# A deeper transpose pipeline in the expert pages of layer 0: four pairs ahead instead of three

## The chip, the cores and the metric

The kernel runs on one core of one Trainium2 chip. The metric is the device time of one execution in microseconds (us). The names of the engines in the profile are PE (TensorE, matrix products), PEld (TensorE's loading of weights), DVE (VectorE), ACT (ScalarE), POOL (GpSimd) and SP (SyncE, which here only issues transfers). Each engine works through its own instructions in order and waits for the others by semaphores.

## What is computed

Two layers, each a graph step over 128 graphs of 64 nodes with 256 features (8192 tokens), followed by a mixture of experts. The change lies in the mixture of layer 0: 64 experts, 6 of them chosen for each token. Cut to that part:

```python
logits = jnp.einsum('bsd,ed->bse', x, gate_w)            # 64 experts
top_logits, indices = jax.lax.top_k(logits, 6)
scores = jax.nn.softmax(top_logits, axis=-1)
W_sel = lattice_weights[indices]                          # (64, 256, 256), one matrix per expert
xW = jnp.einsum('bsd,bskde->bske', x, W_sel)
lattice_out = jnp.einsum('bske,bsk->bse', xW, scores)
# ... then a projection, a residual and a layer norm; layer 1 follows
```

The kernel sorts instead of gathering matrices. While it computes the graph step it writes each token's row six times into a table in HBM (`r0x`), at a place in the chunk of the chosen expert. A row is 258 floats: the 256 features, the row of the answer to which the result belongs, and the score. 128 rows of one expert are a page. A page is read, transposed on TensorE, multiplied by its expert's 256 x 256 matrix (all 64 matrices lie in SBUF as `lat`), scaled by the score and written back by an indirect transfer to the table of answers (`r0y`), from which the next stage sums six rows a token.

## The kernel before

Twelve full pages, one of each of the first twelve experts, are done early, while the last rows of the table are still being sent. Their tiles are placed by hand; the tile named `space` leaves 1008 floats per partition free.

```python
    with tc.tile_pool(name="e0", bufs=1, ...) as ex, tc.tile_pool(name="e1", bufs=4, side="right", ...) as et, ...:
        early = {}
        for j in (0, 3, 2, 1, None, 4, 5):
            if j is None:
                ex.tile([P, 1008], F32, name="space")
            else:
                early[j] = ex.tile([P, 2, W], F32, name=f"early{j}")
        # ... fetch_early, flip_early, apply_early: as below, for the early pages
        for e in range(EARLY):                 # EARLY = 12
            fetch_early(e)
        staggered(EARLY // 2, ((-2, flip_early), (0, apply_early)))
```

Then come all other pages in pairs. `W` is 258, `C` is 256, `KD` is 2. `px` is the buffer of a pair's rows: it takes the fetch, is overwritten by the scaled product, and is free when the reply has read it. `pxT` holds the transposed copy.

```python
    with tc.tile_pool(name="wx0", bufs=3, reuse_waits="tile") as wx, \
            tc.tile_pool(name="pt1", bufs=4, space=PSUM, ...) as pt_pool, \
            tc.tile_pool(name="py1", bufs=4, space=PSUM, ...) as py_pool:
        ring = [wx.tile([P, KD, C], F32, name="pxT", bufs=5)]

        def fetch(j):                          # SyncE
            Q["px"] = px = wx.tile([P, 2, W], F32, name="px", bufs=22)
            for q in range(2):
                # ... the page's row number is loaded once for four pages
                r0.fetch(i, regs["row"][i % 4], px[:, q:q + 1, :])

        def flip(j):                           # TensorE, then ScalarE
            # ... 4 transposes of 128x128 into pt (PSUM)
            Q["xT"] = xT = ring.pop() if ring else wx.tile([P, KD, C], F32, name="pxT", bufs=5)
            nc.scalar.copy(xT[:, :, :n * P], pt[:, :, :n * P])

        def apply(j):                          # TensorE, VectorE, GpSimd
            if j < E0:
                r0.fill_end(j)                 # a write of 128 filler rows, issued by ScalarE
            # ... 8 matmuls of 128x256 into py (PSUM)
            for q in range(n):
                nc.vector.tensor_scalar(px[:, q, :D], py[:, q, :], px[:, q, D + 1:D + 2], None, op0=ALU.mult)
                r0.reply(2 * j + q, px[:, q, :], px[:, q, :D])     # indirect transfer, GpSimd

        stages = ((-12, fetch), (0, apply),
                  (-2, lambda j: flip(j) if j < 4 else None), (-3, lambda j: flip(j) if j >= 4 else None))
        staggered(mean_pages, stages)
        # ... more pairs, if the routing needs them
```

`staggered` runs step s over the stages in the order written: fetch of pair s+12, product of pair s, then transposes of pair s+2 (for the first four pairs) or s+3.

Of the kernel before, what the change touches and what calls it, by code (L numbers as in the profile page):

```python
# [9 lines left out]
F32 = mybir.dt.float32  # L10
# [9 lines left out]
P = 128  # L20
# [445 lines left out]
def staggered(n, stages, first=0):  # L466

    for s in range(first + min(lag for lag, _ in stages), n + max(lag for lag, _ in stages)):
        for lag, f in stages:
            if first <= s - lag < n:  # L470
                f(s - lag)
# [3 lines left out]
def two_layer_gnn_moe_kernel(ctx: ExitStack, tc: tile.TileContext, a: dict, out: bass.AP):  # L475
# [6 lines left out]
    KD = D // P  # L482
    T = 2
    C = T * P
# [75 lines left out]
    W = r0.W  # L560
# [283 lines left out]
    with tc.tile_pool(name="wx0", bufs=3, reuse_waits="tile") as wx, \  # L844
            tc.tile_pool(name="pt1", bufs=4, space=PSUM, reuse_waits="tile") as pt_pool, \
            tc.tile_pool(name="py1", bufs=4, space=PSUM, reuse_waits="tile") as py_pool:
        npair = (r0.pages + 1) // 2
        pairs = [dict() for _ in range(npair)]
        regs = {}
        ring = [wx.tile([P, KD, C], F32, name="pxT", bufs=5)]  # L850

        def fetch(j):
            Q = pairs[j]
            Q["px"] = px = wx.tile([P, 2, W], F32, name="px", bufs=22)
            for q in range(2):
                i = 2 * j + q
                if i % 4 == 0:
                    regs["row"] = r0.load(0, i, ENG.SP)
                if i < r0.pages:
                    r0.fetch(i, regs["row"][i % 4], px[:, q:q + 1, :])  # L860

        def flip(j):
            Q = pairs[j]
            pt = pt_pool.tile([P, KD, C], F32, name="pt")
            n = min(2, r0.pages - 2 * j)
            for q in range(n):
                for k in range(KD):
                    nc.tensor.transpose(pt[:, k, ts(q, P)], Q["px"][:, q, ts(k, P)], ident)  # L868
            Q["xT"] = xT = ring.pop() if ring else wx.tile([P, KD, C], F32, name="pxT", bufs=5)
            nc.scalar.copy(xT[:, :, :n * P], pt[:, :, :n * P])  # L870

        def apply(j):
            Q = pairs[j]
            if j < E0:
                r0.fill_end(j)
            if j % 2 == 0:
                regs["e"] = r0.load(1, 2 * j, ENG.PE)
            py = py_pool.tile([P, 2, D], F32, name="py")
            px, xT = Q["px"], Q["xT"]
            n = min(2, r0.pages - 2 * j)  # L880
            for q in range(n):
                for k in range(KD):
                    nc.tensor.matmul(py[:, q, :], lhsT=xT[:, k, ts(q, P)],  # L883
                                     rhs=lat[:, ds(regs["e"][(2 * j + q) % 4], 1), k, :].rearrange("p o d -> p (o d)"),
                                     start=(k == 0), stop=(k == KD - 1))
            for q in range(n):
                nc.vector.tensor_scalar(px[:, q, :D], py[:, q, :], px[:, q, D + 1:D + 2], None, op0=ALU.mult)  # L887
                r0.reply(2 * j + q, px[:, q, :], px[:, q, :D])


        stages = ((-12, fetch), (0, apply),
                  (-2, lambda j: flip(j) if j < 4 else None), (-3, lambda j: flip(j) if j >= 4 else None))
        likely = (r0.likely_pages - EARLY + 3) // 4 * 2

        mean_pages = (K0 * N // P + E0 // 2 - EARLY) // 4 * 2
        staggered(mean_pages, stages)
        wait = const.tile([1, 4], F32, name="wait")
        with tc.If(r0.needed(2 * mean_pages)):
            staggered(likely, stages, mean_pages)
            with tc.If(r0.needed(2 * likely)):  # L900
                staggered(npair, stages, likely)

                nc.sync.dma_start(out=wait, in_=r0.answer[0:1, 0:4])
# [7 lines left out]
    wx = ctx.enter_context(tc.tile_pool(name="wx1", bufs=2, side="right", reuse_waits="tile"))  # L911
# [317 lines left out]
```

## Time and profile before

| | |
|---|---|
| time, median of three runs | 2074.68 us (2069.03 to 2075.51) |
| span of the profiled execution | 2434.4 us |
| mean granted clock of TensorE in it | 0.927 |
| busy in it: PE, PEld, DVE, ACT, POOL | 84%, 72%, 49%, 41%, 47% |
| stage of layer 0's pages in it (first transpose to last product) | 845.4 to 1469.3 us |
| copies `pxT` / replies `r0y<-px` in that stage | 202 / 404 |

The profiled execution is one run with a recording of every instruction; its span is longer than the time without a recording, so its shares and orders are used, and its sums with care. A line of the costliest groups gives: source line, engine and operation, output<-input, count, then busy time and the mean of one in ns, then the idle time of the engine just before these instructions and what ended most of it. A line of the timeline gives: start, duration, engine, source line, operation, output<-input and count, and in brackets the idle time of the engine before it with its releaser. "issue" means that the profile shows nothing waited for; "remote" that the releaser is not known.

### The profile page before, as it was taken

To read this page: it belongs to the slowest core of one execution; us is meant where nothing else is said; L and a number is where in the kernel's file an instruction comes from. 1 tells how busy PE (TensorE), PEld (TensorE's weight loads), DVE (VectorE), ACT (ScalarE), POOL (GpSimd) and SP (SyncE) were. 2 spreads that over 40 slices of the span, in tenths; PEclk is the share of its full clock that TensorE was granted. 3 is DMA by queue.
4 is the path that set the end of the run, shared out by engine and by line. 5 is a ranking of instruction groups with operands and counts; after the bars stand their busy time and mean duration, and the time that the engine had idled before them with its cause. 6 is when DMAs were issued, how large, how long until landed. Compare 5 with 4: busy or idle time off the path is not lost. (4 is left out here: it accounts for less than half of the span.)

```text
span 2434.4 us, 36827 instructions
## 1 busy us (share of the span) xinstructions
PE 2043.7 (84%) x10516; PEld 1750.1 (72%) x10516; DVE 1184.6 (49%) x3981; ACT 1009.9 (41%) x2033; POOL 1144.3 (47%) x1134
## 2 busy tenths in 40 slices
PE   7887878878876578778787877888988899999997
PEld 6776767767665467666666765777777788888886
DVE  5677657667765622222222224777778422222221
ACT  5765656656655112111111212555555333333332
POOL 0345444554555656666666661233333444444443
PEclk9999889989898689889999888999999899999998
DMA  3223333433234678765555526887774476666665
GB/s 109 91 99 113 125 118 106 131 122 119 101 108 157 196 234 234 218 181 176 174 170 174 160 80 242 289 267 239 248 235 138 128 181 162 162 159 165 160 167 101
DMA packets 282557, 397.88 MB, mean 163 GB/s; under 512 B 56025, under 2 KB 236393, under 8 KB 282353
## 3 DMA queue, kind: packets, MB, share of 16 engines
q1 hardware_dynamic: 202880, 246.61, 34.5%
q0 software_dynamic: 64416, 136.14, 18.8%
q10 hardware_dynamic: 15056, 12.69, 1.6%
q8 instruction: 94, 1.54, 0.3%
q14 instruction: 111, 0.90, 0.1%
HBM read 222.84 MB, written 176.64 MB: 164 GB/s over the span
## 5 line engine op out<-in xcount | busy, mean ns | idle before, releaser
L314 POOL DMA_INDIRECT r0x<-xs,r0row x384 | 385.6, 1004 | 442.3 <-issue 343.3
L883 PE MATMUL py<-lat,pxT 128*128 x1616 | 427.9, 412 | 114.2 <-ACT pxT L870 86.0
L321 POOL DMA_INDIRECT r0y<-px x404 | 392.3, 971 | 230.9 <-DVE px L887 107.2
L883 PEld LDWEIGHTS py<-lat,pxT 128*128 128x128 f32 x1616 | 317.2, 207 | 169.7 <-ACT pxT L870 97.9
L887 DVE TENSOR_SCALAR px<-py,px 128x256 f32<-128x256 f32 x404 | 170.9, 478 | 453.2 <-PE py L883 160.9
L331 POOL DMA_INDIRECT out_x<-py_s,px x138 | 214.6, 1555 | 294.3 <-DMA out_x<-py_s,px 136.8
L870 ACT COPY pxT<-pt 128x512 f32<-128x512 f32 x202 | 113.9, 588 | 515.3 <-remote 161.9
L696 PE MATMUL ps<-lat 128*128 128x256 f32 x1024 | 267.2, 412 | 15.6 <-issue 14.4
L1167 ACT ACTIVATE phid<-ph,pw 128x256 f32<-128x256 f32 x276 | 130.9, 474 | 322.6 <-issue 211.3
L663 PE MATMUL ph<-lat 128*128 128x256 f32 x1024 | 243.8, 396 | 20.6 <-issue 14.3
L1165 PE MATMUL ph<-pxT,pw 128*128 128x256 f32 x1104 | 251.1, 381 | 0.7 <-ACT pxT L1156 0.7
L696 PEld LDWEIGHTS ps<-lat 128*128 128x128 f32 x1024 | 213.1, 211 | 53.5 <-issue 17.9
L1185 PE MATMUL py<-fw,phid 128*128 (+1 forms) x1104 | 249.7, 379 | 0.0
L663 PEld LDWEIGHTS ph<-lat 128*128 128x128 f32 x1024 | 201.1, 199 | 53.6 <-issue 19.4
L1165 PEld LDWEIGHTS ph<-pxT,pw 128*128 128x128 f32 x1104 | 210.7, 191 | 29.9 <-ACT pxT L1156 1.1
L1185 PEld LDWEIGHTS py<-fw,phid 128*128 128x128 f32 x1104 | 204.5, 190 | 25.0
L314 POOL DMA_INDIRECT r1x<-xs,r1row x128 | 126.2, 986 | 202.1 <-DVE bn_rs L1004 114.2
L666 ACT ACTIVATE lat<-ph,c_L_gnn_b 128x256 f32<-128x256 f32 x256 | 102.5, 471 | 113.1 <-remote 52.9
L868 PE MATMUL pt<-ident,px 128*128 128x128 f32 x808 | 132.3, 285 | 7.7 <-issue 7.6
L868 PEld LDWEIGHTS pt<-ident,px 128*128 128x128 f32 x808 | 107.7, 149 | 33.9 <-issue 14.0
L685 DVE SCALAR_TENSOR_TENSOR lat<-ph,c_L_gnn_b,rms 128x256 f32<-128x256 f32 x256 | 103.1, 475 | 52.3 <-ACT rms L59 45.7
L1188 DVE TENSOR_TENSOR py_s<-py,pb 128x512 f32<-128x512 f32 x69 | 47.8, 692 | 155.4 <-PE py L1185 155.4
(303 smaller groups left out, 2872.1 us busy)
## 6 DMA issues: line engine op xcount, KB each, us to landing
px<-r0x SPq DMA_DIRECT2D x404, 129.0 KB
y<-r0y SPq DMA_DIRECT2D x64, 768.0 KB
pw<-in_L_ffn_W1b SPq DMA_DIRECT2D x69, 514.0 KB
px<-r1x SPq DMA_DIRECT2D x69, 258.0 KB
x<-x SPq DMA_DIRECT2D x64, 256.0 KB
pb<-in_L_ffn_b SPq DMA_DIRECT2D x69, 128.0 KB
r0x<-r0filler ACTq DMA_DIRECT2D x64, 129.0 KB
lat<-in_x SPq DMA_DIRECT2D x32, 256.0 KB
```

Of the source, the lines that this page charges most:

```text
L314: i = self.nc.gpsimd.indirect_dma_start(out=self.table[:, :], out_offset=bass.IndirectOffsetOnAxis(ap=row[:, t, k:k + 1], axis=0), in_=xs[ ...
L321: d = self.nc.gpsimd.indirect_dma_start(out=self.answer[:, :], out_offset=bass.IndirectOffsetOnAxis(ap=x[:, self.D:self.D + 1].bitcast(I32 ...
L331: i, d = f"{self.name}add{i}", self.nc.gpsimd.indirect_dma_start(out=self.total[:, :], out_offset=bass.IndirectOffsetOnAxis(ap=x[:, self.D ...
L663: nc.tensor.matmul(ph[:, c, :], lhsT=w1[:, k, ts(2 * j + c, P)], rhs=B["aggT"][:, k, :], start=(k == 0), stop=(k == KD - 1))
L696: nc.tensor.matmul(B["po"][:, t, :], lhsT=B["hT"][:, c, ts(t, P)], rhs=w2[:, c, :], start=False, stop=(t == T - 1 and c == KH - 1))
L868: nc.tensor.transpose(pt[:, k, ts(q, P)], Q["px"][:, q, ts(k, P)], ident)
L870: nc.scalar.copy(xT[:, :, :n * P], pt[:, :, :n * P])
L883: nc.tensor.matmul(py[:, q, :], lhsT=xT[:, k, ts(q, P)], rhs=lat[:, ds(regs["e"][(2 * j + q) % 4], 1), k, :].rearrange("p o d -> p (o d)") ...
L887: nc.vector.tensor_scalar(px[:, q, :D], py[:, q, :], px[:, q, D + 1:D + 2], None, op0=ALU.mult)
L1165: nc.tensor.matmul(ph, lhsT=w[:, k * F1 + c * P:k * F1 + (c + 1) * P], rhs=Q["xT"][:, k, :], start=(k == 0), stop=(k == KD - 1))
L1167: nc.scalar.activation(hid[:, c, :], ph, AF.Relu, bias=w[:, KD * F1 + c:KD * F1 + c + 1], scale=1.0)
L1185: nc.tensor.matmul(py[:, t, :], lhsT=Q["hid"][:, c, ts(t, P)], rhs=fw2[:, ds(e, 1), c, :].rearrange("p o d -> p (o d)"), start=(c == 0), s ...
```

## The change

In the stage of layer 0's pages, pairs from the fifth on are transposed four pairs ahead of their product instead of three. The transposed copies are held longer, so there are seven buffers for them instead of five. The memory comes from the row buffers, 20 pairs instead of 22. It is meant to give the copies on ScalarE more time before TensorE needs them.

```diff
-        ring = [wx.tile([P, KD, C], F32, name="pxT", bufs=5)]
+        ring = [wx.tile([P, KD, C], F32, name="pxT", bufs=7)]
 
         def fetch(j):
             Q = pairs[j]
-            Q["px"] = px = wx.tile([P, 2, W], F32, name="px", bufs=22)
+            Q["px"] = px = wx.tile([P, 2, W], F32, name="px", bufs=20)
...
-            Q["xT"] = xT = ring.pop() if ring else wx.tile([P, KD, C], F32, name="pxT", bufs=5)
+            Q["xT"] = xT = ring.pop() if ring else wx.tile([P, KD, C], F32, name="pxT", bufs=7)
             nc.scalar.copy(xT[:, :, :n * P], pt[:, :, :n * P])
...
         stages = ((-12, fetch), (0, apply),
-                  (-2, lambda j: flip(j) if j < 4 else None), (-3, lambda j: flip(j) if j >= 4 else None))
+                  (-2, lambda j: flip(j) if j < 4 else None), (-4, lambda j: flip(j) if j >= 4 else None))
```

## The prediction

> **What bounds the kernel now.** I read first the costliest groups, to see which engine the page stage of layer 0 leans on.
>
> ```profile
> L883 PE MATMUL py<-lat,pxT 128*128 x1616 | 427.9, 412 | 114.2 <-ACT pxT L870 86.0
> L321 POOL DMA_INDIRECT r0y<-px x404 | 392.3, 971 | 230.9 <-DVE px L887 107.2
> L883 PEld LDWEIGHTS py<-lat,pxT 128*128 128x128 f32 x1616 | 317.2, 207 | 169.7 <-ACT pxT L870 97.9
> L870 ACT COPY pxT<-pt 128x512 f32<-128x512 f32 x202 | 113.9, 588 | 515.3 <-remote 161.9
> ```
>
> The stage runs 202 pairs of pages (202 copies, 404 replies). TensorE loses time to late copies (86.0 us of matmul idle, 97.9 us of weight-load idle, largely the same moments). This is the wait the change goes for. GpSimd's replies wait 107.2 us for VectorE. Next, the timeline of an undisturbed piece gives each engine's period.
>
> ```profile
> 1215.40 0.60 PE L868 MATMUL pt<-ident,px 128*128 128x128 f32 x4
> 1215.84 1.89 PE L883 MATMUL py<-lat,pxT 128*128 x8
> 1217.57 0.60 PE L868 MATMUL pt<-ident,px 128*128 128x128 f32 x4
> ```
>
> And the replies on GpSimd, from the entry of the stage:
>
> ```profile
> 852.14 0.97 POOL L321 DMA_INDIRECT r0y<-early  x1 [0.30 <-issue]
> 853.42 0.97 POOL L321 DMA_INDIRECT r0y<-early  x1 [0.31 <-issue]
> 857.18 0.97 POOL L321 DMA_INDIRECT r0y<-px  x1 [2.80 <-DVE px L887]
> ```
>
> TensorE starts a pair every 1217.57 - 1215.40 = 2.17 us. GpSimd starts a reply every 853.42 - 852.14 = 1.28 us, so a pair costs it 2.56 us. 202 pairs are 438 us of TensorE at full clock and 516 us of GpSimd. Without waits GpSimd is the slower of the two, even against TensorE at the mean granted clock of 0.927 (2.17 / 0.927 = 2.34 us). In the profiled run the stage took 624 us (first transpose 845.4, last product 1469.3), because ScalarE or VectorE sometimes stands still for 5 to 9 us:
>
> ```profile
> 1209.30 0.59 ACT L870 COPY pxT<-pt 128x512 f32<-128x512 f32 x1 [9.09 <-remote]
> 1209.93 3.46 PE L883 MATMUL py<-lat,pxT 128*128 x8 [3.91 <-ACT pxT L870]
> ```
>
> Nothing in the program explains 9.09 us there. The profiled span is 2434.4 us against 2074.68 us timed, so I take most of these stops to be the recording's own. That is a choice, and the prediction hangs on it: late copies then look worth up to about 180 us in the page, but far less in the timed run. They do not concentrate in the part that issues filler writes from ScalarE: TensorE's waits for pxT are 34.2 + 31.1 us in the first 200 us of the stage, 60.6 + 52.6 us in the next 400, the same share.
>
> The last view is the stage's entry.
>
> ```profile
> 838.59 3.22 DVE L836 TENSOR_SCALAR early<-py,early 128x256 f32<-128x256 f32 x8
> ...
> 839.34 0.99 POOL L321 DMA_INDIRECT r0y<-early  x1 [4.36 <-DVE early L836]
> ...
> 839.70 32.19 SPq L460 DMA_DIRECT2D px<-r0x  x28
> ...
> 845.45 0.74 PE L868 MATMUL pt<-ident,px 128*128 128x128 f32 x4
> ...
> 848.15 1.96 PE L883 MATMUL py<-lat,pxT 128*128 x8 [0.42 <-issue]
> ```
>
> The fetches of row buffers start at 839.70, beside the twelve early replies (839.34 to 853.42 + 0.97 = 854.39). So page 0 is transposed at 845.45 and multiplied at 848.15, and GpSimd, done with the early pages at 854.39, finds work prepared; what stops it until 857.18 is a standstill of VectorE.
>
> **What the Trainium skill says.** "Perfetto Trace Analysis", section "DMA Instruction — SWDGE (GPSIMD)": the profiled end is when the descriptors are made, not when the data has landed. So 0.97 us is not the reply; whoever reuses its buffer waits longer. "DMA: Bandwidth & Descriptors", section "Anatomy of one DMA — SWDGE (gpsimd) path": a fixed cost of about 2 us, most of it the receipt from the memory written. No single line here shows the landing of a reply, so I use 2 us as an estimate from that page. "Perfetto Trace Analysis", section "Optimization Strategy": gaps that repeat can mean too few buffers. This trace agrees only in part: the gaps on TensorE repeat, but their releaser is a copy that starts late, not a full ring (waits of the fetches for replies are 19.5 us over 11 times).
>
> **The change part by part.** (1) Transposes from pair 4 on come one pair earlier; no instruction is added or removed. The slack between a transpose and its product grows from three pairs (3 x 2.17 = 6.5 us) to four (8.7 us). A stop of ScalarE of 5 to 9 us is then mostly absorbed. In the timed run I give this 0 to 10 us: TensorE is ahead of GpSimd anyway, and a wait of TensorE costs only if GpSimd has emptied its backlog.
>
> (2) Row buffers 22 to 20. Fetch j+12 waits for the reply of pair j-8 instead of j-10. If GpSimd lags as computed (2.56 against 2.17 to 2.34), TensorE runs ahead until the ring stops it. Each pair of buffers less, and the transpose a pair earlier, shorten the lead it can have by 3 pairs in all, 3 x 2.56 = 7.7 us of lead lost at the end of the stage. The next stage starts when TensorE ends, while GpSimd's last replies are hidden behind its first blocks. Cost 0 to 8 us.
>
> (3) Addresses, which the diff does not show. Seven copies take 7 x 2048 = 14,336 bytes at the start of the pool instead of 10,240. In the built programs the early pages' tiles are laid out so that a gap of 1008 floats stays free. The kernel before puts the row buffer of pair 0 into that gap (address 180,992; the early tiles 4 and 5 start at 183,104 and 185,184), and the buffers that overlap those tiles come only for pairs 12, 14 and 17. In the changed program the copies fill the gap, and the row buffer of pair 0 stands at 185,088, over early tiles 4 and 5. In the order of the built programs the first fetch of a page now waits for VectorE, TensorE and the last four early replies to have landed; the queue of SyncE is in order, so every later fetch waits behind it.
>
> Worked out on the times above: the last early reply has its descriptors at 854.39 and lands at about 856.4, so the first fetch moves from 839.70 to 856.4, 16.7 us later. From issue to the first transpose it takes 845.45 - 839.70 = 5.75 us, from there to the product 2.70, then about 2.2 + 0.6 for the product and its scaling: the first reply starts near 867.7. GpSimd is free at 854.7; it stands 13 us. Next, pair 1 is multiplied only after the transposes of pair 4, which now come before it on TensorE; pair 4 is the ninth fetch, 8 x 1.15 (32.19 / 28) = 9.2 us behind the first, so near 871.4, and the replies of pair 1 begin near 876 instead of 870.3: another 5 to 6 us. From there on fetches (2.3 us a pair) are faster than GpSimd. Sum 18 to 19 us of idle GpSimd, against at most 2.8 in the trace before: about 16 us. TensorE starts about as much later. Whichever of the two sets the end, 16 us stay.
>
> **Sum.** +16 (entry) + 4 (middle of 0 to 8) - 7 (deeper slack, towards the upper end of 0 to 10 because real stops of ScalarE at its filler writes exist: 8.83 us at 913) = +13 us; 2074.7 + 13 = 2088.
>
> **Rivals.** (a) The standstills are real and the deeper transposes win. For it: 184 us of waits for pxT. Removing a third of them would give -30 us net of the entry, 2055 to 2060. Against it: the profiled span is 360 us above the timed one, and behind TensorE comes GpSimd with 516 us that no transposing order shortens. (b) The entry is hidden: if GpSimd's lag is not what ends the stage, or the early replies run later than SyncE's fetch anyway, only a few us remain: 2072 to 2078. Against it: TensorE too has nothing to do until the first page lands. (c) The ring becomes the bound: with 20 pairs and a lag of GpSimd, fetches stop for replies through the whole stage. Each stop costs TensorE, not GpSimd, whose backlog is then full; it stays within the 8 us of part 2, unless landing times under load are much longer than 2 us, then 2100 to 2110.
>
> **Range and chances.** The certain part is +16 with an error of some 5 us; the uncertain ones pull both ways by 10. Three runs of before spread over 6.5 us. I take 2071 to 2104. Two per cent are 41 us: neither way likely. Slower by that needs (c) at its worst on top of the entry, faster needs (a) in full.
>
> **What would show it.** In the changed profile the first fetch of px should start 16 to 20 us after the first early reply, not 0.4 us; GpSimd should show one gap of 12 to 15 us between the last early reply and the first px reply, and a second of about 5 us after pair 0; TensorE's idle for pxT (184 us) should fall, perhaps by half, in the profiled run. If the fetches start beside the early replies as before, part 3 is wrong. If the timed run gains more than 10 us, my taking the standstills for the recording's own is wrong.

## The result and the profile after

The changed kernel takes 2094.44 us (median of four, 2090.5 to 2098.69), the kernel before 2075.1 us: a ratio of 1.010, 95% interval 1.0073 to 1.0128, 19.3 us slower. I had said 2088, within 2071 to 2104.

The costliest groups of the changed kernel that answer to those shown of before:

```profile
L321 POOL DMA_INDIRECT r0y<-px x404 | 393.7, 975 | 134.6 <-issue 45.5
L883 PE MATMUL py<-lat,pxT 128*128 x1616 | 390.2, 385 | 16.9 <-ACT pxT L870 12.4
L870 ACT COPY pxT<-pt 128x512 f32<-128x512 f32 x202 | 117.9, 586 | 386.4 <-PE pt L868 292.1
```

TensorE's matmul idle for late copies has gone from 86.0 us to 12.4 us, and GpSimd's idle from 230.9 to 134.6 us. It looks like the hoped success, with a slower kernel. But the two recordings cannot be compared: their spans are 2434.4 and 2096.9 us, while the times go the other way by 19 us. On which chips these two were made is not known; the experiments show that chips differ by as much. The kernel before, recorded again on a chip where it takes 2076.55 us, has this:

```profile
L321 POOL DMA_INDIRECT r0y<-px x404 | 392.7, 972 | 123.2 <-DMA r0y<-px 51.2
L883 PE MATMUL py<-lat,pxT 128*128 x1616 | 390.5, 385 | 18.1 <-ACT pxT L870 14.0
L870 ACT COPY pxT<-pt 128x512 f32<-128x512 f32 x202 | 118.0, 586 | 368.3 <-PE pt L868 258.2
```

The wait that the change goes for is 14.0 us here, not 86.0. Deeper transposes make it 12.4. GpSimd's idle of 123.2 us is almost all the 0.30 us between one reply and the next (404 x 0.30 = 121); it never waits for work. From here on "before" means this recording. The two recorded runs took 2098.69 and 2076.55 us, so they lie 22 us apart where the medians lie 19.

The entry of the stage, timeline, changed kernel (start, duration, engine, line, operation; in brackets the idle time before):

```profile
675.34 0.98 POOL L321 DMA_INDIRECT r0y<-early  x1 [0.30 <-issue]
678.12 27.01 SPq L460 DMA_DIRECT2D px<-r0x  x40
680.37 2.35 PE L868 MATMUL pt<-ident,px 128*128 128x128 f32 x8 [20.76 <-DMA px<-r0x]
682.87 3.75 PE L883 MATMUL py<-lat,pxT 128*128 x8
687.41 0.97 POOL L321 DMA_INDIRECT r0y<-px  x1 [11.10 <-DMA px<-r0x]
688.69 0.98 POOL L321 DMA_INDIRECT r0y<-px  x1 [0.30 <-issue]
690.47 0.97 POOL L321 DMA_INDIRECT r0y<-px  x1 [0.80 <-DVE px L887]
```

and the kernel before:

```profile
661.53 28.28 SPq L460 DMA_DIRECT2D px<-r0x  x40
663.76 1.19 PE L868 MATMUL pt<-ident,px 128*128 128x128 f32 x4 [4.88 <-DMA px<-r0x]
667.01 3.51 PE L883 MATMUL py<-lat,pxT 128*128 x8
674.39 0.97 POOL L321 DMA_INDIRECT r0y<-early  x1 [0.30 <-DMA r0y<-early]
675.67 0.97 POOL L321 DMA_INDIRECT r0y<-px  x1 [0.30 <-issue]
```

The first fetch is issued at 678.12 instead of 661.53 (1.0 us of this arose earlier, since the first early reply starts at 661.3 instead of 660.3): 1.80 us after the last early reply's descriptors (675.34 + 0.98 = 676.32), which fits a wait for its landing. GpSimd stands 11.10 us where it stood 0.30. The waits of SyncE's own queue in the changed kernel name it (us in total, times, longest); the first line does not occur in the kernel before, the second does there with 181.4 us:

```profile
SPq L460 <- DMA r0y<-early: 15.2, 1, 15.2
SPq L460 <- DMA r0y<-px: 182.8, 133, 3.8
```

The second line is the other thing to see: page fetches wait for replies all through the stage (in the kernel before, 12 to 24 us in every 50 us from 700 to 1150). The ring of row buffers, which are used in turn, is full in both kernels, and GpSimd paces it. The next lines give durations in ns (least, median, longest) and then the start of the first and last product, and of the first and last reply; before, then changed:

```profile
L883 PE MATMUL py<-lat,pxT x1616: 379/379/767, 667.0 to 1144.9; 128*128 x180
L321 POOL DMA_INDIRECT r0y<-px x404: 967/970/1250, 675.7 to 1190.3; - x135
```

```profile
L883 PE MATMUL py<-lat,pxT x1616: 379/379/763, 682.9 to 1165.7; 128*128 x180
L321 POOL DMA_INDIRECT r0y<-px x404: 968/972/1234, 687.4 to 1203.7; - x135
```

Replies come every (1190.3 - 675.7) / 403 = 1.277 us before and (1203.7 - 687.4) / 403 = 1.281 us after. GpSimd ends 13.4 us later, TensorE 20.8 us later. TensorE's lead at the end (start of the last reply less that of the last product) is 1190.3 - 1144.9 = 45.4 us before and 38.0 us after. The next stage starts with TensorE: its first matmul moves from 1151.5 to 1171.6, and the last stage's first from 1545.5 to 1567.6. Two losses, then: the entry, and 7.4 us of lead.

### The profile page after: what moved, and what is told of

The parts are those of the page before. It is cut to its first block, busy times and chain, and to the rows that moved or that the text cites. A ratio compares the mean times of both kernels' runs of the same rounds, so it can differ in the third digit from the quotient of the medians.

```text
span 2096.9 us, 36822 instructions
## 1 busy us (share of the span) xinstructions
PE 1935.8 (92%) x10516; PEld 1679.1 (80%) x10516; DVE 1187.0 (57%) x3981; ACT 1016.9 (48%) x2033; POOL 1159.8 (55%) x1134
## 5 line engine op out<-in xcount | busy, mean ns | idle before, releaser
L314 POOL DMA_INDIRECT r0x<-xs,r0row x384 | 395.7, 1031 | 258.1 <-issue 171.1
L321 POOL DMA_INDIRECT r0y<-px x404 | 393.7, 975 | 134.6 <-issue 45.5
L883 PE MATMUL py<-lat,pxT 128*128 x1616 | 390.2, 385 | 16.9 <-ACT pxT L870 12.4
L887 DVE TENSOR_SCALAR px<-py,px 128x256 f32<-128x256 f32 x404 | 177.0, 480 | 329.5 <-PE py L883 325.6
L883 PEld LDWEIGHTS py<-lat,pxT 128*128 128x128 f32 x1616 | 294.1, 192 | 58.2 <-ACT pxT L870 16.3
L663 PE MATMUL ph<-lat 128*128 128x256 f32 x1024 | 234.1, 388 | 11.6 <-DVE lat L685 10.9
L696 PE MATMUL ps<-lat 128*128 128x256 f32 x1024 | 237.4, 380 | 0.0
L696 PEld LDWEIGHTS ps<-lat 128*128 128x128 f32 x1024 | 193.1, 191 | 24.6
L868 PEld LDWEIGHTS pt<-ident,px 128*128 128x128 f32 x808 | 100.8, 143 | 58.1 <-issue 26.2
L1179 DVE TENSOR_SCALAR p<-p 128x2 f32<-128x2 f32 x69 | 11.7, 170 | 225.5 <-ACT p L1178 225.5
L687 ACT ACTIVATE lat<-lat,c_L_gnn_rms_weight 128x256 f32<-128x256 f32 x256 | 105.7, 495 | 37.7 <-DVE lat L685 37.3
```

Source lines behind the costliest of these rows:

```text
L314: i = self.nc.gpsimd.indirect_dma_start(out=self.table[:, :], out_offset=bass.IndirectOffsetOnAxis(ap=row[:, t, k:k + 1], axis=0), in_=xs[ ...
L321: d = self.nc.gpsimd.indirect_dma_start(out=self.answer[:, :], out_offset=bass.IndirectOffsetOnAxis(ap=x[:, self.D:self.D + 1].bitcast(I32 ...
L663: nc.tensor.matmul(ph[:, c, :], lhsT=w1[:, k, ts(2 * j + c, P)], rhs=B["aggT"][:, k, :], start=(k == 0), stop=(k == KD - 1))
L696: nc.tensor.matmul(B["po"][:, t, :], lhsT=B["hT"][:, c, ts(t, P)], rhs=w2[:, c, :], start=False, stop=(t == T - 1 and c == KH - 1))
L883: nc.tensor.matmul(py[:, q, :], lhsT=xT[:, k, ts(q, P)], rhs=lat[:, ds(regs["e"][(2 * j + q) % 4], 1), k, :].rearrange("p o d -> p (o d)") ...
```

## The experiments

My theory: the loss is the late entry plus the shorter lead, and the deeper transposes bring nothing, because TensorE is ahead of GpSimd. Rivals: the ring costs all of it; or the deeper transposes do gain, under a larger loss.

**The chips.** The first runs fell on a chip where the kernel before takes 2449 us. The kernel before, recorded there:

> The kernel before, unchanged, recorded once more. Theory (the standstills of ScalarE and VectorE were the recording's own): a recording without them shows a span near 2075 us, TensorE's waits for pxT under 40 us, GpSimd's replies 1.28 us apart through the whole stage, the first page fetch 0 to 3 us after the first early reply's start, and a gap of GpSimd between the last early reply and the first px reply under 3 us. Rival (the kernel before really stands still, and the deeper transposes cured it): waits for pxT near 180 us again.

```profile
L883 PE MATMUL py<-lat,pxT 128*128 x1616 | 426.5, 411 | 115.0 <-ACT pxT L870 89.7
L870 ACT COPY pxT<-pt 128x512 f32<-128x512 f32 x202 | 113.3, 589 | 516.9 <-remote 170.6
```

Its span was 2447.3 us, and 47 timed runs of the kernel before on this chip gave 2449.15 us (2440.56 to 2460.14). TensorE's waits for `pxT` were 89.7 us in the matmuls and 102.4 us in the weight loads, near 180 as the rival said; but these are waits of the unchanged kernel, and whether the deeper transposes cure them is another question. On another chip the expectation was

> The kernel before, unchanged, recorded in the hope of a chip on which it takes 2075 us. Theory: there the recording shows a span near 2075 us, TensorE's waits for pxT under 40 us, replies of GpSimd 1.28 us apart through the whole stage, fetches of pages beside the early replies, a gap of GpSimd before the first px reply under 1 us. Rival: waits for pxT of 100 us and more, as on the other chip.

and it held: span 2074.8 us, first fetch 1.2 us after the start of the first early reply (660.3), and the groups shown above. So a recording takes as long as the timed runs of its chip, and it does not make the standstills: they went with the chip. Of the four chips of these experiments two gave 2075 us to the kernel before and two 2449 us. I compare only within a chip, with one exception that is named.

**The entry given back.** The changed kernel, with more space left free among the early tiles:

```diff
-                ex.tile([P, 1008], F32, name="space")
+                ex.tile([P, 2024], F32, name="space")
```

> The changed kernel with the space among the early tiles made 2024 floats, once more, in the hope of a chip on which the kernel before takes 2075 us. There, theory (late entry most, shorter lead the rest): 2081 to 2086, fetches beside the early replies, GpSimd without a gap. Rival (the ring costs all): 2092 to 2097. Rival (the deeper transposes gain): 2070 or below. On a chip where the kernel before takes 2449 us: no difference over 0.3%, as the first time.

2083.06 us against 2076.6: ratio 1.0031 (1.0021 to 1.0042). The first fetch is at 661.60, and GpSimd goes straight on:

```profile
674.25 0.97 POOL L321 DMA_INDIRECT r0y<-early  x1 [0.30 <-DVE px L887]
675.53 0.97 POOL L321 DMA_INDIRECT r0y<-px  x1 [0.30 <-DMA r0y<-early]
```

```profile
L883 PE MATMUL py<-lat,pxT x1616: 379/379/767, 667.2 to 1152.2; 128*128 x180
L321 POOL DMA_INDIRECT r0y<-px x404: 967/970/1242, 675.5 to 1190.2; - x135
```

GpSimd ends where it ended before (1190.2), and TensorE's lead is still 38.0 us. Of the ratio 1.010, 1.0100 / 1.0031 = 1.0069 is the entry, about 14 us; 0.0031, 6.5 us, is left. This is the exception: the two ratios were not measured side by side, and with their intervals the entry is 8 to 20 us. GpSimd's end, 13.4 us later in the changed kernel and not later here, agrees. That rules out the ring as the whole cause, and leaves the deeper transposes no gain larger than what the rows cost.

On the chip of 2449 us the same kernel gave no difference, 0.9989 (0.997 to 1.0009):

> The changed kernel with the hand-placed space among the early tiles made 2024 floats instead of 1008, so that the row buffer of pair 0 lies over no early tile; transposes four ahead, seven copies, 20 rows as changed. Theory (the late entry is most of the loss, the shorter lead the rest): about 11 us of the 19 come back, 2081 to 2086; first page fetch beside the early replies again. Rival (the shorter ring costs all of it): 2092 to 2097. Rival (the deeper transposes gain something that the entry hid): 2070 or below.

There the question of the rival was best posed, since there TensorE does wait for copies. Little of the wait is now put to the copies (15.5 us), but most of the idle time is still there:

```profile
L883 PE MATMUL py<-lat,pxT 128*128 x1616 | 432.3, 407 | 91.8 <-issue 73.9
```

The matmul idle is 91.8 us instead of 115.0, and the time is the same within -7 to +2 us. GpSimd's idle before its replies hardly moved (235.8 us against 237.0).

**The entry alone.** The kernel before without the space, so that pair 0 lies over early tiles 4 and 5:

```diff
-        for j in (0, 3, 2, 1, None, 4, 5):
+        for j in (0, 3, 2, 1, 4, 5):
```

> The kernel before with the space among the early tiles taken out, so that the row buffer of pair 0 lies over early tiles 4 and 5; three ahead, five copies, 22 rows as before. Theory (late entry): 11 to 14 us slower than before, 2086 to 2089, with a gap of GpSimd of about 11 us after the last early reply. Rival (the ring costs all): 2075, as before.

> The kernel before with the space taken out (pair 0 over early tiles 4 and 5), again, where the kernel before takes 2075 us. Theory (the late entry alone): 12 to 14 us slower than before, first page fetch about 16.6 us after its place in the kernel before, GpSimd standing 11 us, the lead of TensorE at the stage's end unchanged at 45 us. Rival (entry and lead are not additive): under 8 us or over 18.

Both fell on chips of 2449 us: ratios 1.0029 (1.0013 to 1.0045) and 1.0015 (1.0003 to 1.0027), 4 to 7 us slower. The wait and the gap themselves are as expected: SyncE's first page fetch waits 15.8 us for an early reply in both recordings, and GpSimd stands (first run)

```profile
852.64 0.97 POOL L321 DMA_INDIRECT r0y<-early  x1 [0.31 <-issue]
864.88 0.97 POOL L321 DMA_INDIRECT r0y<-px  x1 [11.27 <-DVE px L887]
```

That less than the gap reaches the end fits a GpSimd that waits anyway on these chips (237.0 us of idle before its replies in the kernel before, against 123.2 us). The number for a chip of 2075 us was not measured; there the entry's cost rests on the changed kernel with and without the wider space.

**The rows alone.** The kernel before with `px` at `bufs=20` instead of 22:

> The kernel before with 20 pairs of row buffers instead of 22 and nothing else. Theory (a pair of row buffers is 2.56 us of lead of TensorE over GpSimd at the end of the stage): 5 us slower, 2079 to 2081. Rival (the ring never fills): 2075. Rival (the ring costs all): 2090 or more.

That was the chip of 2449 us: 1.0005 (0.9991 to 1.0018), nothing. On a chip of 2075 us:

> The kernel before with 20 pairs of row buffers instead of 22 and nothing else, again. On a chip at 2075 us, theory (two pairs of 2.56 us less lead of TensorE over GpSimd at the stage's end): 4 to 6 us slower than before. Rival (the loss left in the version with the wider space comes from the deeper transposes and copies alone): no difference.

2083.96 against 2075.55 us, ratio 1.0039 (1.0028 to 1.005), 8.4 us. More than expected, and enough for all of what the wider space left over (6.5 us; the intervals overlap).

```profile
L883 PE MATMUL py<-lat,pxT x1616: 378/379/764, 667.8 to 1150.4; 128*128 x180
L321 POOL DMA_INDIRECT r0y<-px x404: 967/969/1201, 676.3 to 1191.7; - x135
```

The lead falls from 45.4 to 41.3 us, by 4.1 us, near two pairs less (2 x 2.55 = 5.1). TensorE ends 5.5 us later than before, and the last stage starts 8.5 us later (1554.0 us against 1545.5; with the wider space it starts at 1554.0 us too). So some 3 us arise in the stage between; why, these runs do not show.

**The depth alone.** Four ahead with six copies and all 22 row buffers, space at 1512 floats so that the entry stays early:

```diff
-                ex.tile([P, 1008], F32, name="space")
+                ex.tile([P, 1512], F32, name="space")
...
-                  ... (-3, lambda j: flip(j) if j >= 4 else None))
+                  ... (-4, lambda j: flip(j) if j >= 4 else None))
```

> Four pairs ahead with six copies and all 22 row buffers, the space among the early tiles at 1512 floats so that the row buffer of pair 0 lies over no early tile. Theory (a transpose one pair earlier is one pair, 2.56 us, less lead of the products; nothing is gained, since TensorE is ahead of GpSimd): 1 to 4 us slower than before. Rival (the deeper transposes gain, and only the rows cost): 3 us or more faster than before.

2076.61 against 2075.55 us, ratio 1.0002 (0.9992 to 1.0011): nothing within some 2 us either way. TensorE's wait for copies is 12.0 us here, 14.0 before:

```profile
L883 PE MATMUL py<-lat,pxT 128*128 x1616 | 388.9, 384 | 15.6 <-ACT pxT L870 12.0
```

The last product starts 1.9 us later (1146.8 against 1144.9), as one more product behind the last transpose would.

**The opposite direction.** Two ahead, four copies, 24 row buffers, early tiles in the order 0, 1, 2, 3 and a pad of 32 floats so that pair 0 stays free:

> The opposite direction: all pairs two ahead, four copies, 24 pairs of row buffers, with early tiles placed so that pair 0 lies over none of them. Theory (lead at the stage's end is rows less transposes ahead: three pairs more than before): 5 to 8 us faster than before, TensorE's end of the stage that much nearer. Rival (copies two pairs ahead come too late, above all while ScalarE issues the filler writes): slower than before by 5 us or more.

2073.98 against 2075.55 us, ratio 0.9994 (0.9982 to 1.0006): not the 5 to 8 us. TensorE's last product starts 3.6 us earlier (1141.3), but GpSimd ends later, at 1198.0: it stands for pages or products not yet there at four places of the early part (6 us together, the first of them here) and once before its last reply:

```profile
690.60 0.97 POOL L321 DMA_INDIRECT r0y<-px  x1 [1.82 <-DMA px<-r0x]
1197.97 1.07 POOL L321 DMA_INDIRECT r0y<-px  x1 [5.15 <-DVE bn_mv L46]
```

What held the last reply is not settled; VectorE is by then in the next stage. What the longer lead runs into can be seen. The kernel lets only the first five blocks of the next stage read answers before the last reply has landed, and SyncE's fetch for the sixth block waits for it (before, then two ahead; the line number is shifted by one):

```profile
SPq L939 <- DMA r0y<-px: 5.6, 1, 5.6
SPq L940 <- DMA r0y<-px: 16.2, 1, 16.2
```

That fetch starts at 1200.31 us instead of 1193.93, although TensorE ends its pages earlier. So GpSimd's last replies are not wholly hidden, even in the kernel before. Whether this wait took up the expected gain is not shown: the last stage still starts at 1544.9 us, against 1545.5.

**A version meant to beat both.** Three ahead as before, four copies, 24 row buffers, placed as in the last one:

> Three pairs ahead as before, but four copies instead of five and 24 pairs of row buffers instead of 22, with early tiles placed so that pair 0 lies over none. Theory (20 to 22 pairs was worth 8 us, one pair ahead or less under 2): TensorE ends the stage 5 us nearer, 5 to 8 us faster than before. Rival (22 pairs are enough, or four copies make the transposes wait): no difference or slower.

> Three pairs ahead, four copies, 24 pairs of row buffers, again, in the hope of a chip on which the kernel before takes 2075 us. There, theory (each pair of row buffers is lead of TensorE over GpSimd): TensorE's last product 5 us nearer, 2067 to 2070, 5 to 8 us faster than before. Rival (22 pairs are enough, or the hidden tail of GpSimd comes to light in the next stage once the lead is longer): 2073 to 2078.

Both runs fell on chips of 2449 us: 0.9991 (0.9979 to 1.0002) and 1.0011 (0.9996 to 1.0025), no difference. As 20 rows showed none there either, this says nothing of a chip of 2075 us. Whether two more pairs help is open.

## Why the prediction was right, and where it was not

- **What bounds the stage.** Right: GpSimd, 2.55 us a pair against TensorE's 2.17. On a chip of 2075 us its replies follow each other after 0.30 us, in the changed kernel as before; there only the two gaps of the entry stand out (11.10 and 0.80 us). The order of the transposes adds and removes no reply.
- **The standstills.** I took them for the recording's own. Wrong: they went with the chip, and the long span of the first recording, which I put down to the recording, with them. For the times given at the start, which at 2075 us leave no room for them, the consequence drawn was still right. The sign I had named, a fall of the pxT wait "perhaps by half", came out and more (184 to 29 us in both idle sums together, which count largely the same moments), and meant nothing: the unchanged kernel has 32 us on such a chip. A view that changes as foretold is no evidence when the two recordings are not of the same conditions.
- **The entry (+16).** Right in mechanism and near in size. The first fetch was issued 1.80 us after the last early reply's descriptors, where I had estimated 2 us for the landing from the Trainium skill, "DMA: Bandwidth & Descriptors", section "Anatomy of one DMA — SWDGE (gpsimd) path". It moved 16.6 us for 16.7, 1.0 us of it from before the stage. GpSimd's first gap was 11.10 for 13: the first transpose follows the fetch by 2.25 us and not 5.75, while from the first product to the first reply it took 4.54 us and not 2.8. The second gap, "another 5 to 6 us" for pair 1, failed: it was 0.80 us. The fetches follow each other every 27.01 / 40 = 0.68 us, not 1.15, so pair 4 was there in time. GpSimd ended 13.4 us later; by the runs with and without the wider space the entry is about 14 us (8 to 20).
- **The rows (+4, the middle of 0 to 8).** The mechanism was right, and so was the lead lost: 7.4 us for the 7.7 computed. The cost was undersized, since nearly all of it reached the end: the two pairs alone measured 8.4 us; with the depth, the rest after the entry was 6.5 us. The ring is full through the whole stage even in the kernel before, which the first recording, with 19.5 us of such waits, did not show.
- **The deeper slack (-7).** This is the step that failed: "towards the upper end of 0 to 10 because real stops of ScalarE at its filler writes exist". They exist (in the kernel before ScalarE stands 5.79 us before the copy at 716.14, directly behind a filler write), but TensorE makes them up before GpSimd runs dry. The depth alone measured +1 us, within some 2 us of nothing. The prediction's own part (1) had the reason: a wait of TensorE costs only if GpSimd has emptied its backlog. The -7 went against it.
- **A rival's figure.** "-30 us net of the entry, 2055 to 2060" does not close: 2074.7 - 30 is 2045. The range fits roughly a gain of 30 us with the entry's 16 taken off it.

So 16 + 4 - 7 = 13 should have been 14 + 6.5 + 0, about 20, against 19.3 measured (the 14 is what the 6.5 leaves, so that this sum closes is no proof of its own). The two errors of the smaller terms pointed the same way, and the range held the result because the entry, the largest term, was near. A range of 33 us, which holds the 2075.1 us of the kernel before too, proves little; the late first fetch and GpSimd's gap, foretold and found near their figures, prove more.

## What to carry to other kernels

Before a pipeline is made deeper, ask whether the engine that waits is the one that paces the stage: here TensorE waited for copies, but GpSimd set the pace, and its backlog swallowed the waits. Buffers that change size also change addresses; look in the built program at what the first buffer of a stage now lies over, since one wait at the head of an in-order queue (15.2 us here) delays all that stand behind it. When two recordings differ in span by more than the times do, record the unchanged kernel again beside the changed one before reading anything from the difference.

## What the runs showed of the hardware

The same program took 2075 us on two chips and 2449 us on two others, steadily (29 runs at 2071.09 to 2080.33 on one, 47 at 2440.56 to 2460.14 on another). One of the slower two, used twice, gave 2449.15 and 2452.27 us. On the slower ones ScalarE and VectorE stand still again and again, with a releaser that the profile cannot name: ScalarE's copies 30 times (170.6 us in all, up to 11.4 at a time), VectorE's scalings 28 times (141.1 us, up to 8.9), in the kernel before recorded there. Effects that measure about 8 and 14 us on the others shrink or vanish. The cause of the standstills is not known. The granted clock does not explain it alone: 0.927 there and 0.973 here differ by a factor of 1.05, the times by 1.18.
